# A graph layer with 640 hot edges of 1608 a part instead of 512 of 1532, and gathers that wait for a weighted copy three parts in front

## The chip, the cores and the metric

The kernel runs on one core of a Trainium2 chip. The metric is device time in microseconds (us) of one execution, and the number for a kernel is the median of three runs. The core has TensorE (PE, with its weight loads PEld), VectorE (DVE), ScalarE (ACT), GpSimd (POOL) and SyncE (SP); each takes its instructions in order. DMAs are issued from the queues of SP and POOL in what follows.

## The reference, cut to what matters

There are 12500 nodes with 128 features, and 412500 edges (`src`, `dst`), sorted by `dst`.

```python
theta = x[dst] - x[src]
w = sigmoid(relu(theta @ W1 + b1) @ W2 + b2)          # one gate an edge
agg = segment_sum(w * theta, dst)
indeg = segment_sum(ones, dst)
out = layernorm(x + agg + indeg * (x @ W4 + b4))
```

## The kernel before, in words

**Tables.** First a table `z` of 256 columns a node is written to DRAM: `x @ W1` and `x`. The edges are then taken in parts, in the order of `dst`. The first 18 parts (`PLAIN`) are of 1024 edges, whose rows are all gathered. Each later part has `CE` = 1532 edges, up to 1024 of them *cold* and up to 512 of them *hot*. Two parts make a block `b`; part `s` is half `h = s % 2` of block `s // 2`. There are 258 parts behind the plain ones, 18 to 275.

**Cold edges.** POOL gathers their rows of `z` with eight indirect DMAs of 128 rows a part (L401), into one of five buffers `zbuf`. DVE subtracts them from `y`, the rows of the destinations that PE has spread over the edges by a one-hot product (`spread_y`, L893, L951), multiplies by W2 (L956) and sums (L962). ACT makes the gate (L975) and the weighted copies into `wx` (L993).

**Hot edges.** The nodes up to 8192 are cut into 32 regions of 256 rows, four to a group. From each region a part takes at most 8 edges for each of its two lists, 512 in all, and their rows are not gathered but made by PE: DVE builds a one-hot tile `of` from the edges' places (`hot_tiles`, L1039), and PE multiplies it with three bf16 terms of the region's rows, which stay in SBUF (`hot_products`, L1055, 24 products for eight parts of a group). ACT copies the sums into a ring `xT` (`hot_out`, L1069). For part `t` PE then turns `xT` and adds the destinations' rows (`hot_turned`, L1105, L1106: 512 columns in the bank `pz`), ACT takes relu (L1111), PE makes the gates' sums with `hr` as weights and one column moving (`hot_rows`, L1119) and transposes `xT` (L1122), and ACT makes gates and weighted copies `wxh` (`hot_weights`, L1128, L1131).

**Sums.** PE adds cold and hot edges into a window of 104 nodes by one-hot products (L1158): `begin_block` in an odd part, `add_block` in an even one, which also takes the hot edges of both halves. `total`, `finish`, `own` and `normalize` close a block; the square root of the variance is taken for five blocks together (`LB`, L1269).

**Which edges are hot** is found on the chip (`place`, L500): for 64 parts together, DVE runs 32 rounds, one a region, each an eight-wide maximum and a replacement over lists of 767 numbers (L586, L589), and then sorts the rest together. It is a generator whose steps are fitted in behind the parts' own work by a credit (2.5 a part, 5.5 a plain part).

**Order.** The main loop `part(s)` writes PE, ACT, DVE and SP's instructions in the order in which they run; nothing reorders them. In part `s` PE does `hot_turned(s+1)`, `spread_y(s+2)`, `hot_rows(s+1)`, and then the block's sums and the 24 hot products in turns (`issue`). The gathers of part `s+3` are issued in `spread_ahead(s)`, and write the buffer that part `s-2` has left. `paced` is looked up by `gather` but is empty.

Of the kernel before, what the change touches and what calls it, by code (L numbers as in the profile page):

```python
# [9 lines left out]
F32 = mybir.dt.float32  # L10
# [10 lines left out]
P = 128  # L21
# [15 lines left out]
NW = 3  # L37
AHEAD = 4
LB = 5
# [11 lines left out]
HK = HR * HS  # L51
HQ = HK // P
HOT = P * HT
LEADS = tuple(range(8))
OPENING = ((0,), (1, 7), (2, 6), (3, 5), (4,))
NU = 4
# [7 lines left out]
CE = 1532  # L64
# [5 lines left out]
HKL = HR * HE  # L70
# [14 lines left out]
def gnn_resnorm(  # L85
# [49 lines left out]
    assert HK == P * G and 2 * AW + D + WB <= 512 and LW <= SW  # L135
# [65 lines left out]
    of_buf = const.tile([P, max(HT * RG * HB * HS, BE)], F32, name="of")  # L201
    of_half = [of_buf.bitcast(BF16)[:, i * HT * RG * HB * HS:(i + 1) * HT * RG * HB * HS] for i in range(2)]
# [32 lines left out]
    wx_buf = [const.tile([P, K, AW], F32, name=f"wx{i}") for i in range(NW)]  # L235

    def table_load(c):
        n0, np_, m = chunks[c]
        xt = wx_buf[c % NW].rearrange("p k d -> p (k d)")[:, :BE]
# [15 lines left out]
    for name, v in (("w2_r", W2), ("b4_r", b4)):  # L255
        rows[name] = const.tile([P, D], F32, name=name)
        nc.sync.dma_start(
            rows[name], bass.AP(tensor=v.tensor, offset=v.offset, ap=[[0, P], [1, D]]))
# [11 lines left out]
    iota_row = const.tile([P, P], F32, name="iota_row")  # L270
# [36 lines left out]
    for i, t in enumerate(y2_buf):  # L307
        nc.vector.memset(t, 0.0)
        for h in range(SUB) if i < NY else (1,):
# [44 lines left out]
    xT_all = const.tile([P, HX, HK], F32, name="xT")  # L354
    xT_flat = xT_all.rearrange("p j e -> p (j e)")
# [7 lines left out]
    assert late_at + 2 * NS <= HX * HK and WB + D <= 512  # L363
    hot_src = const.tile([P, NU, RG * HB * HS], F16, name="hot_src")
# [135 lines left out]
    def place(i, scratch, es, ed, bb, dp):  # L500
# [79 lines left out]
        tops = ep.tile([P, WL], F32, name="ed")[:, :HKL].rearrange("p (r e) -> p r e", e=HE)  # L580
        for r in range(HR):
# [3 lines left out]
            eight = tops[:, r, :]  # L585
            v.max(eight, left)  # L586
            v.tensor_scalar(eight, eight, FLOOR, None, op0=OP.max)
            yield "k"
            v.match_replace(left, eight, left, TAKEN)  # L589
            yield "k"  # L590
# [19 lines left out]
        yield "p"  # L610
        hrel = pp.tile([P, S2, HQ], BF16, name="hrel")
        pt = scratch()[:, :HQ * P].rearrange("p (q j) -> p q j", q=HQ)
        for q in range(HQ):
            nc.tensor.matmul(pt[:, q, :], hd[:, q * P:(q + 1) * P], ident_b, start=True, stop=True)
        yield "c"
        for q in range(HQ):
            for h in range(LISTS):
                a, e = max(h * HKL - q * P, 0), min((h + 1) * HKL - q * P, P)
                if a < e:
                    nc.scalar.activation(hrel[a:e, :, q], pt[a:e, q, h * S2:(h + 1) * S2], AF.Copy)  # L620
        hot_s = dram.tile([HR // RG, S2, LISTS, RG * HE], F16, name=f"hot_s{i}")
        rows_d = dram.tile([S2, RW], BF16, name=f"off_d{i}")
        for h, at in enumerate(lists):
            nc.sync.dma_start(hot_s[:, :n, h, :].rearrange("g p e -> p g e"),
                              hi[at].rearrange("p (g e) -> p g e", e=RG * HE))
            nc.sync.dma_start(
                rows_d[:n, BP:].rearrange("p (l m) -> p l m", l=LISTS)[:, h, :], far[at])
        hots[s0] = hot_s, hrel, n
        yield "s"
# [89 lines left out]
    with tc.manual_schedule(engines={SP}), tc.tile_pool(name="work", bufs=2) as wp, tc.tile_pool(  # L719
# [65 lines left out]
        def load_block(b):  # L785
            base = nc.values_load(base_b[0:1, b:b + 1], engines=[SP], min_val=0, max_val=N - WB,
                                  skip_runtime_bounds_check_because="base_b is at most N - WB")
            xw = wp.tile([P, D], F32, name="xw", bufs=5)
# [4 lines left out]
            if PLAIN <= b * SUB < PLAIN + NY * SUB:  # L793
                nc.vector.memset(y2[HALF:], 0.0)
            x2 = blocks[b]["x2"] = y2 if b >= W0 else x2_buf[b]
            for h in range(SUB):
# [5 lines left out]
                nc.sync.dma_start(to[h * HALF:h * HALF + SW, :], rows)  # L802
            if b * SUB >= PLAIN:
# [3 lines left out]
                for h in range(SUB):  # L807
                    nc.sync.dma_start(
                        to_all[h * HALF:(h + 1) * HALF, :],
                        rows_d[i + h:i + h + 1, :].to_broadcast([HALF, RW]))  # L810
# [71 lines left out]
        def spread_y(s):  # L882
# [3 lines left out]
            for k0 in range(0, K if s < PLAIN else J, J):  # L886
# [4 lines left out]
                d["y"].append(y)  # L891
                for j in range(J if s < PLAIN else pairs(s)):
                    nc.tensor.matmul(y[:, j, :], d["oh"][:, (k0 + j) * P:(k0 + j + 1) * P],  # L893
                                     y_of(s), start=True, stop=True)
# [73 lines left out]
        def lgh():  # L968

            return halves[1][:, :SUB * HQ].rearrange("p (i q) -> p i q", q=HQ)  # L970
# [41 lines left out]
        EP = RG * HS  # L1012
# [20 lines left out]
        def hot_tiles(f, x=0):  # L1033

            i0, g, i1, i = f
            w = (i1 - i0) * HS * RG
            of = hot_of(turn_of[0] % 2, x, w)
# [4 lines left out]
        def hot_products(f, x, pd, steps_of):  # L1042

            i0, g, i1, i = f
            w = (i1 - i0) * EP
            of = hot_of(turn_of[0] % 2, x, w)
            of = of.rearrange("p t (m r e) -> p t r m e", r=RG, e=HE)
            if not x:
                pd = ps_l.tile([P, G, P], F32, name="pd").rearrange("p g e -> p (g e)")
            bank, pd = pd, pd[:, x:x + w]  # L1050
            to = pd.rearrange("p (m r e) -> p r m e", r=RG, e=HE)
            for q in range(RG):
                for j in range(HT * TERMS):
                    i, t = divmod(j, HT)
                    steps_of.append(lambda q=q, i=i, t=t, j=j: nc.tensor.matmul(  # L1055
                        to[:, q], tabs[:, g, i, q, t, :], of[:, t, q], start=j == 0, stop=j == HT * TERMS - 1))
            return bank, pd

        def hot_out(f, pd):
# [699 lines left out]
```

## Time and profile before

| | |
|---|---|
| median of 3 runs | 2937.81 us (2935.55 to 2943.02) |
| profiled execution's own time | 2943.8 us |
| its span, first to last instruction | 2942.0 us |
| busy PE, DVE, ACT, POOL | 87%, 81%, 72%, 74% of the span |
| mean granted TensorE clock | 0.937 |

A line of the page's groups and of the list by line has: line, engine, operation, tiles out<-in, shapes, count | busy us, mean ns of one | idle time of the engine before it and what ended that. A line of the timeline has: start in us, length in us, engine, line, operation, tiles, shapes, count, and in brackets the idle time before it. A busy PE is not a PE at its peak: the ends of matmuls are modelled, so the starts of two groups tell better what a group takes. Each f32 matmul stands as two passes, a transpose as one.

### The profile page before, as it was taken

The numbers are of one execution on the slowest core, as the hardware profiler recorded it, in microseconds if no ns is written. First come the engines' busy times: TensorE is split into PE (matmuls) and PEld (weight loads), VectorE is DVE, ScalarE is ACT, GpSimd is POOL, SyncE is SP. The second block draws the span as 40 slices with busy tenths as digits, with TensorE's granted clock in tenths as the row PEclk, the third lists the DMA queues.
The fourth block names the chain that finished last, engine by engine and source line by source line (L and its number), as shares of the span: only waits on it lengthen the run. The fifth ranks groups of instructions, "written<-read, shape, count | busy, mean of one in ns | idle before, by whom it ended". The sixth has DMA issues, their size and how long they took to land.

```text
span 2942.0 us, 59129 instructions
## 1 busy us (share of the span) xinstructions
PE 2548.2 (87%) x18606; PEld 2012.3 (68%) x18606; DVE 2380.3 (81%) x4436; ACT 2123.8 (72%) x6416; POOL 2164.5 (74%) x2213
## 2 busy tenths in 40 slices
PE   6877899988888998998898888898998888888886
PEld 5656677777676777776776666676776666677764
DVE  7899699888957988888558888888568888888654
ACT  6365778767777777677777777776777777677776
POOL 4566777777777777777777777777777777777774
PEclk8688999989999999999999999999999999999998
DMA  8455555555554555554554545454554555555542
GB/s 285 151 153 123 142 139 138 140 135 137 140 146 134 137 140 140 133 141 135 143 150 133 135 133 141 132 141 134 143 142 128 140 132 141 133 138 141 141 134 77
DMA packets 239329, 413.58 MB, mean 141 GB/s; under 512 B 63423, under 2 KB 147226, under 8 KB 237470
## 3 DMA queue, kind: packets, MB, share of 16 engines
q0 software_dynamic: 105280, 286.93, 35.3%
q1 hardware_dynamic: 131756, 116.40, 15.3%
q10 hardware_dynamic: 1970, 6.40, 0.7%
q8 instruction: 148, 2.42, 0.3%
q14 instruction: 175, 1.43, 0.2%
HBM read 388.57 MB, written 20.94 MB: 139 GB/s over the span
## 4 chain that ended last, share of the span: by engine, by line
PE 38%; ACT 19%; DVE 15%; DMA 11%; issue 7%; POOL 1%; DVEq 0%; SPq 0%; ACTq 0%; POOLq 0%
PE pa L1158 14%; DMA zbuf<-z,src_i 10%; DVE zbuf L951 5%; PE y L893 5%; PE pd L1055 5%; ACT wx L993 5%; PE px L1119 4%; ACT wxh L1131 4%; PE pz L1105 3%; PE pz L1106 3%; PE pz L1122 3%; ACT oh L872 2%; ACT oh L873 2%; ACT xT L1069 1%; ACT a L1213 1%
## 5 line engine op out<-in xcount | busy, mean ns | idle before, releaser
L401 POOL DMA_INDIRECT zbuf<-z,src_i x2060 | 2018.5, 980 | 637.0 <-issue 236.6
L993 ACT ACTIVATE wx<-zbuf,wx 128x128 f32<-128x128 f32 x2060 | 630.2, 388 | 0.0
L1158 PE MATMUL pa<-wx,ow 128*104 128x260 f32 (+1 forms) x2284 | 628.4, 393 | 0.0
L893 PEld LDWEIGHTS y<-y,oh 128*128 128x128 f32 (+1 forms) x2156 | 276.1, 197 | 420.5 <-DVE zbuf L951 378.2
L1055 PEld LDWEIGHTS <-tabs 128*128 128x128 bf16 x6360 | 452.8, 101 | 124.2 <-issue 8.2
L951 DVE TENSOR_TENSOR zbuf<-y,zbuf 128x1024 f32<-128x1024 f32 x258 | 315.1, 1221 | 272.2 <-DMA zbuf<-z,src_i 270.9
L1055 PE MATMUL pd<-of,tabs 128*128 128x128 bf16 (+3 forms) x6360 | 535.2, 223 | 0.0
L1111 ACT ACTIVATE hr<-pz 128x512 f32<-128x512 f32 x258 | 152.9, 593 | 522.9 <-PE pz L1106 522.8
L893 PE MATMUL y<-y,oh 128*128 128x128 f32 (+1 forms) x2156 | 314.7, 291 | 228.7 <-DVE zbuf L951 220.6
L1158 PEld LDWEIGHTS pa<-wx,ow 128*104 128x104 f32 x2284 | 342.8, 179 | 40.6 <-issue 0.4
L962 DVE TENSOR_REDUCE lg<-zbuf 128x8 f32<-128x1024 f32 x273 | 329.8, 1208 | 13.2
L956 DVE SCALAR_TENSOR_TENSOR zbuf<-zbuf,fix 128x1024 f32<-128x1024 f32 x273 | 331.6, 1215 | 9.3
L1158 PE MATMUL pa<-wxh,owh 128*104 128x130 f32 x2064 | 329.0, 296 | 0.0
L1131 ACT ACTIVATE wxh<-pz,wxh 128x128 f32<-128x128 f32 x1032 | 295.2, 369 | 42.1 <-PE pz L1122 35.9
L1105 PE MATMUL pz<-xT,wni 128*128 128x512 f32 x516 | 278.5, 621 | 1.6 <-ACT wxh L1131 1.6
L1158 PEld LDWEIGHTS pa<-wxh,owh 128*104 128x104 f32 x2064 | 274.3, 186 | 0.0
L1119 PEld LDWEIGHTS px<-w_c,hr 128*128 128x128 f32 x2064 | 263.5, 200 | 7.8 <-ACT hr L1111 7.8
L1119 PE MATMUL px<-w_c,hr 128*128 128x1 f32 x2064 | 262.1, 248 | 5.6 <-ACT hr L1111 5.6
L1106 PE MATMUL pz<-oh,y 128*128 128x512 f32 x516 | 264.5, 594 | 0.1
L872 ACT ACTIVATE oh<-to_all,away,mine 128x512 f32<-128x512 bf16 (+1 forms) x257 | 213.6, 831 | 3.1 <-DMA to_all<-off_d 3.1
L1106 PEld LDWEIGHTS pz<-oh,y 128*128 128x128 f32 x516 | 98.2, 191 | 124.3 <-issue 123.4
L1122 PE MATMUL pz<-wni,xT 128*128 128x128 f32 x1032 | 176.3, 297 | 0.0
(304 smaller groups left out, 3595.8 us busy)
## 6 DMA issues: line engine op xcount, KB each, us to landing
to_all<-off_d SPq DMA_DIRECT2D x258, 128.0 KB
zbuf<-z,src_i POOLq DMA_INDIRECT x2060
hot_src<-hot_s SPq DMA_DIRECT2D x228, 128.0 KB
y<-z SPq DMA_DIRECT2D x270, 28.0 KB
xw<-in_x_dram SPq DMA_DIRECT2D x138, 52.0 KB
out_dram<-o SPq DMA_DIRECT2D x138, 52.0 KB
wx<-in_x_dram ACTq DMA_DIRECT2D x12, 512.0 KB
z<-zbuf SPq DMA_DIRECT2D x6, 1024.0 KB
```

The source lines that it names most:

```text
L401: ins = nc.gpsimd.indirect_dma_start(out=rows_of(s)[:, k, :], out_offset=None, in_=z if s >= NH else x, in_offset=IndirectOffsetOnAxis(ap= ...
L893: nc.tensor.matmul(y[:, j, :], d["oh"][:, (k0 + j) * P:(k0 + j + 1) * P], y_of(s), start=True, stop=True)
L951: nc.vector.tensor_sub(half, yy.to_broadcast([P, 2, n, D]), half)
L956: nc.vector.scalar_tensor_tensor(h[:, at, :], h[:, at, :], 0.0, w2.to_broadcast([P, n, D]), op0=OP.max, op1=OP.mult)
L962: nc.vector.tensor_reduce(lg[:, at, 0], h[:, at, :], AX.X, OP.add)
L993: weighed[0] = nc.scalar.activation(wx[:, k, :D], rows_of(s)[:, k, D:], AF.Copy, scale=wx[:, k, D:D + 1])
L1055: steps_of.append(lambda q=q, i=i, t=t, j=j: nc.tensor.matmul(to[:, q], tabs[:, g, i, q, t, :], of[:, t, q], start=j == 0, stop=j == HT * ...
L1105: nc.tensor.matmul(pz, wneg, xT, start=True, stop=False)
L1106: nc.tensor.matmul(pz, y_of(t), blocks[t // SUB]["oh"][:, BP:], start=False, stop=True)
L1119: nc.tensor.matmul(lgh()[:, t % SUB, q:q + 1], hr[:, at], w2_c, start=True, stop=True)
L1131: nc.scalar.activation(wx[:, q, :D], pz[:, q * P:(q + 1) * P], AF.Copy, scale=wx[:, q, D:D + 1])
L1158: return [lambda i=i, one=one, w=w: nc.tensor.matmul(to if len(w.shape) == 3 else to[:, 0, :], one, w, start=first and i == 0, stop=last a ...
```

## The change

`CE` goes from 1532 to 1608. One region in four has a second round of maxima, so a group has 5 instead of 4 times 8 places a list (`RU`), and a part 640 instead of 512 hot places (`HK`, five columns of 128 instead of four, `HQ`). There are 246 parts behind the plain ones (18 to 263) instead of 258, and four calls of `place` instead of five.

What follows from 640 columns, which no longer fit one bank of 512: `hot_turned` works on two banks of 320, and its destinations' rows come by two products of 64 rows each; relu is two instructions; the gates' sums are made with W2 spread over 32 columns as weights and `hr` moving, so that they lie in rows (`rowed`); a sigmoid over 256 columns and two transposes turn them back (`hot_gates`, `hot_gates_turned`), and ACT copies them out before the weighted copies. The second round's region has products of 256 instead of 128 columns, the last region lies in another bank and is copied by itself (`last_out`). `spread_y` uses 64 rows instead of 128 with zeros. The sums and the hot products no longer take turns. One region's list is longer, so `place` has 40 rounds over lists of 805. Buffers shrink to make room: `wx` 3 to 2, `hot_src` 4 to 3, `owh` 2 to 1, `xw` 5 to 4, `LB` 5 to 4.

The gathers of part `s+3` are issued at the end of part `s` and the first of the eight waits for ACT's last weighted copy of part `s` (`paced`); the other seven no longer wait for ACT themselves.

```diff
-CE = 1532
+CE = 1608
-HK = HR * HS
+HK = HR // RG * RU * HS
+ST = 32
...
-            eight = tops[:, r, :]
+            for _ in range(1 if r % RG else 2):
+                eight = tops[:, u, :]
...
-                nc.sync.dma_start(to[h * HALF:h * HALF + SW, :], rows)
+                for g in range(SUB) if b * SUB >= PLAIN else (h,):
+                    nc.sync.dma_start(to[g * HALF:g * HALF + SW, :], rows)
...
+                if s >= PLAIN:
+                    at = slice(s % SUB * HALF, (s % SUB + 1) * HALF)
+                    oh, rows = oh[at], rows[at]
...
-            nc.tensor.matmul(pz, wneg, xT, start=True, stop=False)
-            nc.tensor.matmul(pz, y_of(t), blocks[t // SUB]["oh"][:, BP:], start=False, stop=True)
+            banks = pz[:, :HKL], halves[1][:, :HKL]
+            for l, to in enumerate(banks):
+                nc.tensor.matmul(to, wneg, xT[:, l * HKL:(l + 1) * HKL], start=True, stop=False)
+            for l, to in enumerate(banks):
+                at = slice(l * HALF, (l + 1) * HALF)
+                nc.tensor.matmul(to, y_of(t)[at], oh[at], start=False, stop=True)
...
-                nc.tensor.matmul(lgh()[:, t % SUB, q:q + 1], hr[:, at], w2_c, start=True, stop=True)
+                nc.tensor.matmul(rowed(q), w2_c.to_broadcast([P, ST]), hr[:, at], start=True, stop=True)
...
+            nc.scalar.activation(parts[t]["hr"][:, :2 * P], pz[:, 2 * P:], AF.Sigmoid, bias=b2_c)
...
+            nc.tensor.transpose(pz[:, 2 * P:3 * P], gates[:, :P], ident)
+            for q in range(G, HQ):
+                at = slice((q - G) * ST, (q - G + 1) * ST)
+                newest[0] = nc.tensor.transpose(pz[:, 2 * P + q * ST:2 * P + (q + 1) * ST],
+                                                gates[at, P:2 * P], ident[at, at])
...
+            if PLAIN + AHEAD <= s + 3 < NS:
+                paced[s + 3] = weighed[0]
+                gather(s + 3)
```

On PE, in an odd part, from the turned hot edges to the first hot product; `pz`, `px`, `y` and `pd` are PSUM tiles, `wni` holds the negative W1 and the identity, `w_c` is W2, `tabs` the regions' terms. Before:

```order
L1105 MATMUL pz<-xT,wni 128x512
L1106 MATMUL pz<-oh,y_146 128x512
L893 MATMUL y<-y_149,oh 128x128 x4
L1119 MATMUL px<-w_c,hr 128x1 x4
L1122 MATMUL pz<-wni,xT 128x128 x4
L1170 LDWEIGHTS third
L1170 MATMUL pa<-b_t,third 104x128
L1171 MATMUL pa<-wts,xuT 104x128
L815 MATMUL pa<-wni,xw 128x104
L1158 MATMUL pa<-wx_78,ow 104x260
L1055 LDWEIGHTS tabs
```

Now:

```order
L1136 MATMUL pz<-xT,wni 128x320
L1136 MATMUL px<-xT,wni 128x320
L1139 MATMUL pz<-oh,y_147 128x320
L1139 MATMUL px<-oh,y_147 128x320
L910 MATMUL y<-y_142,oh 128x128 x4
L1153 MATMUL pz<-hr,w_c 32x128 x5
L1156 MATMUL pz<-wni,xT 128x128 x2
L1156 MATMUL px<-wni,xT 128x128 x3
L1082 LDWEIGHTS tabs
L1082 MATMUL pd<-of,tabs 128x16x16
```

The hot part works on two banks, the gates' products give 32 rows each, and all 24 hot products now stand ahead of the block's sums. Also on PE, what stands now between the last hot product and the next part (the two transposes of the gates, and an odd part's sums):

```order
L1082 MATMUL px<-of,tabs 128x128
L1165 MATMUL pz<-wni,hr 128x128
L1168 MATMUL pz<-wni,hr 128x32
L1216 LDWEIGHTS third
L1216 MATMUL pa<-b_t,third 104x128
L1217 MATMUL pa<-wts,xuT 104x128
L828 MATMUL pa<-wni,xw 128x104
L1205 MATMUL pa<-wx_78,ow 104x260 x4
L1136 MATMUL pz<-xT,wni 128x320
```

Only these sums lie between the gates' transposes and the next part's first product into the same bank. On ACT, in an odd part, from the hot gates to the next part's relu. Before:

```order
L1128 ACTIVATE wxh<-px,b_c 128x4
L1131 ACTIVATE wxh<-pz,wxh 128x128 x4
L1232 ACTIVATE sw<-a 104x2
L1234 ACTIVATE px<-xw,sw 104x128
L975 ACTIVATE wx_78<-lg,b_c 128x8
L979 ACTIVATE wx_78<-rel 128x4
L993 ACTIVATE wx_78<-zbuf_176,wx_78 128x128 x8
L1111 ACTIVATE hr<-pz 128x512
```

Now:

```order
L1175 ACTIVATE wxh<-pz 128x5
L1178 ACTIVATE wxh<-pz,wxh 128x128 x2
L1178 ACTIVATE wxh<-px,wxh 128x128 x3
L1097 ACTIVATE xT<-px 128x12x8
L1097 ACTIVATE xT<-px 128x4x8
L1278 ACTIVATE sw<-a 104x2
L1280 ACTIVATE xw<-xw,sw 104x128
L996 ACTIVATE wx_79<-lg,b_c 128x8
L1000 ACTIVATE wx_79<-rel 128x4
L1014 ACTIVATE wx_79<-zbuf_178,wx_79 128x128 x8
L1097 ACTIVATE xT<-pd 128x12x32
L1097 ACTIVATE xT<-pd 128x4x32
```

The relu follows behind these; one weighted copy and the four copies of hot sums have come ahead of it.

More of the change, by code (lines that the diff above doesn't have):

```diff
@@ L1156, in products @@
         def products(to, terms, first, last):
-            return [lambda i=i, one=one, w=w: nc.tensor.matmul(
-                to if len(w.shape) == 3 else to[:, 0, :], one, w,
-                start=first and i == 0, stop=last and i == len(terms) - 1) for i, (one, w) in enumerate(terms)]
+            for i, (one, w) in enumerate(terms):
+                newest[0] = nc.tensor.matmul(to if len(w.shape) == 3 else to[:, 0, :], one, w,
+                                             start=first and i == 0, stop=last and i == len(terms) - 1)
         def sums_of(b):
@@ L1185, in add_up @@
                 terms.append((blocks[b]["sh"][:WB, :WB], carry[0][:WB, :AW]))
-            issue(products(blocks[b]["pa"][:, 1:, :], terms, h == 0 and begin, h == 1 and end), [])
+            products(blocks[b]["pa"][:, 1:, :], terms, h == 0 and begin, h == 1 and end)
             if end:
```

231 lines of the change are left out of this document (133 added, 98 removed).

## The prediction

> **What bounds the kernel now.** I read the page's groups first, then the timeline of POOL, the windows, the waits, and the timelines of PE and ACT over two parts. The group that the page puts first is POOL's:
>
> ```profile
> L401 POOL DMA_INDIRECT zbuf<-z,src_i x2060 | 2018.5, 980 | 637.0 <-issue 236.6
> ```
>
> The timeline of POOL, in the main loop and in the plain parts, shows what its idle time is:
>
> ```profile
> 1448.38 0.95 POOL L401 DMA_INDIRECT zbuf<-z,src_i  x1 [0.30 <-issue]
> 1449.63 0.95 POOL L401 DMA_INDIRECT zbuf<-z,src_i  x1 [0.30 <-issue]
> ...
> 166.69 0.95 POOL L401 DMA_INDIRECT zbuf<-z,src  x1 [0.30 <-issue]
> 167.95 0.95 POOL L401 DMA_INDIRECT zbuf<-z,src  x1 [0.30 <-issue]
> ```
>
> Gathers start 1.25 us apart, 0.95 and then 0.30 that belong to every issue. With the mean of the group it is 0.98 + 0.30 = 1.28, and eight make 10.24 us a part. The windows agree, with DVE light or heavy and the clock low or full:
>
> ```profile
> 100.00:200.00 100.00, 79.01 (x376) 60.30 (x375) 92.55 (x191) 54.71 (x133) 66.99 (x65) 0.76 0.50 138
> ...
> 1500.00:1600.00 100.00, 85.42 (x614) 67.75 (x613) 67.40 (x129) 72.66 (x224) 76.22 (x78) 0.91 0.53 143
> 1600.00:1700.00 100.00, 87.35 (x679) 67.80 (x678) 89.65 (x154) 76.44 (x237) 76.84 (x77) 1.00 0.52 137
> ```
>
> (The pairs are PE, PEld, DVE, ACT, POOL; then the granted clock.) POOL issues 77 or 78 in 100 us whatever the others do: it never waits. The others wait for it, in the list of waits:
>
> ```profile
> PEld y L893 <- DVE zbuf L951: 378.2, 197, 9.7
> DVE zbuf L951 <- DMA zbuf<-z,src_i: 270.9, 138, 6.5
> ```
>
> The length of a part comes from the first and last start of the hot edges' first product, which stands once a part:
>
> ```profile
> L1105 PE MATMUL pz<-xT,wni x516: 591/594/1057, 290.3 to 2911.1; 128*128 128x512 f32 x172
> ```
>
> That is (2911.1 - 290.3) / 257 = 10.20 us, POOL's own pace. Outside these 257 intervals lie 2942.0 - 2620.8 = 321.2 us. So POOL bounds the main loop, and PE is the next: two parts in which it never waited, from the timeline of PE:
>
> ```profile
> 1518.08 1.08 PE L1105 MATMUL pz<-xT,wni 128*128 128x512 f32 x2
> 1518.99 1.02 PE L1106 MATMUL pz<-oh,y 128*128 128x512 f32 x2
> 1519.85 1.05 PE L893 MATMUL y<-y,oh 128*128 128x128 f32 x8
> 1520.74 1.01 PE L1119 MATMUL px<-w_c,hr 128*128 128x1 f32 x8
> 1521.61 0.63 PE L1122 MATMUL pz<-wni,xT 128*128 128x128 f32 x4
> 1522.09 0.39 PE L1158 MATMUL pa<-a,sh 104*104 104x130 f32 x2
> ...
> 1525.17 1.95 PE L1158 MATMUL pa<-wx,ow 128*104 128x260 f32 x8
> 1526.96 0.50 PE L1055 MATMUL pd<-of,tabs 128*128 128x128 bf16 x6
> 1527.29 1.08 PE L1105 MATMUL pz<-xT,wni 128*128 128x512 f32 x2
> ...
> 1531.37 0.22 PE L1170 MATMUL pa<-b_t,third 65*104 65x128 bf16 x1
> ...
> 1531.77 0.60 PE L1158 MATMUL pa<-wx,ow 128*104 128x260 f32 x2
> ...
> 1534.97 1.08 PE L1105 MATMUL pz<-xT,wni 128*128 128x512 f32 x2
> ```
>
> An even part takes 9.21 us and an odd one 7.68, 8.45 in the mean, at full clock by the window of these two:
>
> ```profile
> 1518.00:1535.00 17.00, 17.00 (x140) 13.82 (x137) 9.05 (x15) 12.06 (x39) 12.75 (x14) 1.00 0.70 173
> ```
>
> PE has 1.8 us a part to spare; the change is paid out of that. Where PE waits long the clock is granted lower (0.91 above). I count full clock, since these waits should go.
>
> **The change part by part.** *Twelve parts fewer.* 245 intervals instead of 257: at the old pace 12 x 10.20 = 122 us less. POOL's floor stays: the gathers of the plain parts above wait for one semaphore alone and are 1.26 us apart too, so dropping ACT's wait from seven of eight gains nothing.
>
> *PE a part*, from the starts above, at full clock. A pass of 512 columns takes 0.43, so one of 320 takes 0.27. Turned rows: 4 x 0.27 + 0.05 = 1.13 for 0.91, **+0.22**. Destinations' rows: 4 x 0.27 = 1.08 for 0.86, **+0.22**. Gates' sums: ten passes of 128 columns at 0.11 (0.89 for the eight of L893) for 0.87, **+0.23**. A fifth transpose (four take 0.48) **+0.12**, two for the gates **+0.17**. Hot products: six of 24 have 256 columns, 0.11 for 0.055 (six take 0.33, 1526.96 to 1527.29), **+0.33**; that they no longer take turns with the sums costs nothing, since they run at 0.055 in the groups above already. Hot sums: four passes more a block at 0.11, **+0.22** a part. Then the array changes its shape five times a part: full to 64 rows, to 32 columns, to full, to 32 rows, to full. Before it never does in the main loop, but in the first plain parts it does so at every matmul:
>
> ```profile
> 119.21 0.49 PE L917 MATMUL y<-wni,xT 128*128 128x128 f32 x2
> 119.62 0.49 PE L915 MATMUL y<-y,oh 64*128 64x128 f32 x2
> ```
>
> Two passes take 0.41 until the next pair starts instead of 0.22, so one change costs 0.19, and five **+0.95**. The row is of 64 against 128 rows; the 32-wide forms I price by it, as the nearest there is. The Trainium skill, "TensorEngine Tiling (Array Packing)", Key Properties, says that every change of tiling mode drains TensorE, not only this one. By that rule all five are paid; by the row alone two of them are, and the part would be 0.57 us shorter.
>
> The sum is +2.46: 10.91 us a part if everything on PE runs one behind the other. Two places can be shorter: the destinations' products use different halves of the array's rows, and the gates' sums different quarters of its columns. If one tile's first pass runs beside its neighbour's second, these are 3 and 6 steps: 0.81 and 0.66, together 0.71 less, 10.20. No row of before has two tiles side by side, so both stay as ends.
>
> *ACT*, which PE waits for. Here is an odd part's second half in the timeline of ACT:
>
> ```profile
> 1530.16 0.67 ACT L1069 ACTIVATE xT<-pd 128x192 f32<-128x192 f32 x2
> 1530.69 0.84 ACT L872 ACTIVATE oh<-to_all,away,mine 128x512 f32<-128x512 bf16 x1
> ...
> 1532.70 0.25 ACT L1128 ACTIVATE wxh<-px,b_c 128x4 f32<-128x4 f32 x1
> 1532.98 1.14 ACT L1131 ACTIVATE wxh<-pz,wxh 128x128 f32<-128x128 f32 x4
> 1533.99 0.22 ACT L1232 ACTIVATE sw<-a 104x2 f32<-104x2 f32 x1
> ...
> 1534.55 0.29 ACT L975 ACTIVATE wx<-lg,b_c 128x8 f32<-128x8 f32 x1
> ...
> 1534.88 2.45 ACT L993 ACTIVATE wx<-zbuf,wx 128x128 f32<-128x128 f32 x8
> 1537.23 0.57 ACT L1111 ACTIVATE hr<-pz 128x512 f32<-128x512 f32 x1
> ```
>
> In the changed order the weighted copies cannot start before the gates are turned back, and behind them stands all of this before the next relu. From the last gates' transpose on PE: 0.16 until its result is there (1518.99 + 1.02 against 1519.85), 0.28 gates, five copies at 0.25 = 1.26, last hot sums 0.20 (by the 0.53 of L1069 for 512 columns), 0.56 and 0.33 for own and gate, 2.35 for eight copies, 0.53 hot sums, relu of 640 columns 0.70: 6.37. PE meanwhile has, in an odd part, a change of shape 0.19, 0.40 (1531.37 to 1531.77), 1.79 of sums, then 1.13 + 0.19 + 1.08 or 0.81, 0.89 and 0.19: 5.86 or 5.59, and then needs the relu. It waits 0.51 or 0.78 a pair of parts, **0.26 or 0.39** a part. Behind an even part the sums are 2 us longer, and there is no wait. The square root comes on the same path:
>
> ```profile
> 1458.63 1.28 ACT L1269 ACT_TABLE_LOAD   x1
> ...
> 1460.13 0.58 ACT L1111 ACTIVATE hr<-pz 128x512 f32<-128x512 f32 x1
> ```
>
> 1.50 us, now once in four blocks, eight parts: **+0.19**. Before, the wait for POOL hid it.
>
> So a part is 10.91 + 0.26 + 0.19 = 11.36 us one behind the other, and 10.20 + 0.39 + 0.19 = 10.78 with overlap. I take 10.9, near the second: tiles on different rows or columns share no cell.
>
> *DVE* gets eight rounds more a call of `place`, from the list by line:
>
> ```profile
> L586 DVE MAX8 ed<-ew 128x8 f32<-128x767 f32 x160 | 153.1, 957 | 4.3 <-PE px L762 0.3
> L589 DVE MATCH_REPLACE8 ew<-ed,ew 128x767 f32<-128x767 f32 x160 | 150.6, 941 | 0.0
> ```
>
> 8 x (0.96 + 0.94 + 0.3 of small ones) = 17.6, and lists 5% longer some 6 more: 24 us a call. The first call stands in the plain parts, where DVE is 93% busy: **+24 us** on the path. Later calls are spread over some 57 parts, DVE then stands near 9.2 us a part, under 10.9. The lower end for the 24 is 0.
>
> *Free.* The wait of the gathers, on POOL, where only later gathers queue behind it. An odd part's subtraction on DVE's timeline, and a gather's landing in the chain that ended last:
>
> ```profile
> 1526.83 1.22 DVE L951 TENSOR_TENSOR zbuf<-y,zbuf 128x1024 f32<-128x1024 f32 x1 [4.97 <-DMA zbuf<-z,src_i]
> ...
> 1533.52 2.79 DMA zbuf<-z,src_i
> ```
>
> That part's copies end at 1537.23, 10.4 us behind its subtraction. The subtraction three parts on comes 30.6 us behind it at POOL's pace; less 2.8 of landing and 10.2 of gathers, POOL comes to those gathers 17.6 us behind it. The wait costs nothing until ACT is 7 us later than now. SP gets four more DMAs a block; DMA engines stand at 0.53, loads have two parts in hand, and nothing but output queues behind them. Fewer buffers of `wx`, `owh`, `hot_src` each leave about a part of room.
>
> *Sum.* 321.2 + 24 + 245 x 10.9 = 3016 us of span, +2.5% on 2942.0. The profiled execution's own time is 1.8 us over its span and 0.2% over the median: 3011 us.
>
> **Rivals.** (1) *PE fits under POOL*: tiles run wholly side by side and the 32-wide changes cost little. Then 10.24 rules, 321 + 24 + 245 x 10.24 = 2854, 2850 on the median's scale: 3% faster. It decides when PE with its waits is under 10.24, that is 0.54 below my lower sum. For it: the 0.95 for changes rests on one kind of row. Against it: ACT's chain gets longer relative to PE whenever PE gets shorter, so that 0.55 less on PE gains only some 0.3. Chance 0.20. The Trainium skill, "TensorE: Matmul & The Clock Gate", Part 3, gives the span of packed tiles as one matmul and some 4 ns a tile. By that rule the two places are 0.54 and 0.44 and the part 10.43, some 2897 us; no row here shows it. (2) *In between*, 10.35 to 10.63 a part, 2880 to 2945: 0.12, of which 0.05 is within 0.3% (about what a measurement can tell from no change; 10.56 to 10.63). (3) *Worse*: the 32-column tiles cannot load weights ahead and each pass takes 0.21, as the first pass behind a change does now: +1 us a part, 3260. Chance 0.06. (4) Too many edges of a part do not fit, and the kernel falls back on its general branch behind the flag: far slower, and no trace prices it. 0.02.
>
> **How the numbers follow.** Forecast (10.63 to 11.4) 0.60, and the rivals 0.20, 0.12, 0.06, 0.02. Faster: 0.20 + 0.07 = 0.27; same 0.05; slower 0.60 + 0.08 = 0.68. The range goes from rival 1 at 2850 to 11.4 us a part at 3135. The forecast's own is 2945 to 3135.
>
> **What would show it.** Right: POOL idle between groups of eight, not only 0.30 a gather; PE's waits for L951 gone and waits for relu in every second part; PE's clock nearer 1; 0.41 for two passes behind each change of shape; the first hot product near 314 us. Wrong: POOL still at 78 in 100 us (rival 1), or gates' sums over 1.5 us (rival 3).

## The result and the profile after

The changed kernel takes 3086.4 us (median of 4 runs, 3081.6 to 3093.4), the kernel before beside it 2939.5: a ratio of 1.0502 (95% interval 1.0479 to 1.0526), slower, twice the 2.5% that the forecast of 3011 us stood for. The profiled execution's own time is 3093.4 us, its span 3091.6. Twelve of the eighteen experiments' runs fell on chips where TensorE was granted less clock and the kernel before itself took 4037 to 4122 us; a ratio is always to the kernel before on the same chip.

The length of a part again comes from the first and last start of the hot edges' first product (here L1136), from the list by source line; then POOL's gathers, from the groups by shape:

```profile
L1136 PE MATMUL pz<-xT,wni x492: 432/432/741, 333.1 to 3060.5; 128*128 128x320 f32 x164
```

```profile
L405 POOL DMA_INDIRECT zbuf<-z,src_i x1962 | 1884.6, 961 | 884.3 <-issue 516.9 <-ACT wx L1014 306.7 <-ACT src_i L723 19.7
```

(3060.5 - 333.1) / 245 = 11.13 us a part, where the forecast has 10.9. The main loop takes 2727.4 us, 106.6 more than before, the stretch ahead of it 42.8 more (333.1 against 290.3), the tail the same 31. A gather still takes 0.96 + 0.30; POOL no longer sets the pace. The windows show where the time is (pairs of PE, PEld, DVE, ACT, POOL, then the granted clock): with `place` running, right behind it, and in the last 71 parts, where there is no `place` to do:

```profile
1500.00:1600.00 100.00, 88.64 (x684) 70.47 (x684) 78.11 (x131) 74.50 (x237) 64.69 (x69) 0.90 0.48 129
1600.00:1700.00 100.00, 91.95 (x739) 73.06 (x737) 58.77 (x96) 85.03 (x278) 73.64 (x78) 0.98 0.53 142
1700.00:1800.00 100.00, 61.47 (x462) 48.41 (x461) 45.60 (x94) 55.16 (x176) 46.58 (x48) 0.80 0.34 95
2400.00:2500.00 100.00, 93.61 (x766) 74.35 (x764) 59.92 (x96) 83.82 (x274) 74.31 (x79) 0.98 0.54 146
```

In the rows without `place` POOL issues 78 or 79 gathers in 100 us, as before the change; in the first, with it, 69. Taken by part, from the starts of L1136: 141 parts in which `place` works on VectorE take 11.46 us in the mean, the last 71 take 10.42. The third row holds one stall of 26.5 us. The list of waits names the engine:

```profile
DVE a L1270 <- ACT xuT L833: 408.8, 109, 8.2
POOL zbuf L405 <- ACT wx L1014: 306.7, 141, 29.2
PEld y L910 <- DVE zbuf L968: 272.3, 120, 10.1
PE y L910 <- DVE zbuf L968: 211.3, 120, 9.6
```

```profile
PE pz L1153 <- ACT hr L1145: 33.4, 30, 2.7
...
DVE zbuf L968 <- DMA zbuf<-z,src_i: 11.3, 29, 1.5
```

PE's wait for VectorE's subtraction is there as before, but the subtraction no longer waits for a gather (11.3 us, 270.9 before): VectorE itself is late. `finish` (L1270) waits for `total` on ACT 408.8 us, 51.6 before:

```profile
DVE a L1224 <- ACT xuT L820: 51.6, 21, 6.3
```

VectorE's timeline over a pair of parts with `place` (L968 is a part's subtraction, L689 the first of a place step, L1298 begins `normalize`):

```profile
1502.85 1.22 DVE L968 TENSOR_TENSOR zbuf<-y,zbuf 128x1024 f32<-128x1024 f32 x1
...
1511.04 1.21 DVE L968 TENSOR_TENSOR zbuf<-y,zbuf 128x1024 f32<-128x1024 f32 x1
...
1519.45 0.29 DVE L1270 TENSOR_TENSOR a<-a,pa 104x130 f32<-104x130 f32 x1 [4.12 <-ACT xuT L833]
1519.66 1.24 DVE L1187 TENSOR_TENSOR owh<-fix,hrel 128x1040 f32<-128x1040 f32 x1
...
1521.40 0.69 DVE L689 TENSOR_SCALAR px<-ew 128x512 int32<-128x512 int32 x1
...
1524.98 0.28 DVE L1298 TENSOR_TENSOR xw<-xw,a 104x128 f32<-104x128 f32 x1
...
1526.39 1.22 DVE L968 TENSOR_TENSOR zbuf<-y,zbuf 128x1024 f32<-128x1024 f32 x1
```

From 1502.85 to 1526.39 is 23.54 us, 11.8 a part. The first window below is this stretch, the second the time right behind the wait of TensorE that is shown next:

```profile
1502.85:1526.39 23.54, 22.27 (x156) 17.75 (x156) 18.80 (x33) 12.93 (x47) 13.11 (x14) 0.81 0.41 113
1504.10:1508.00 3.90, 3.88 (x22) 3.21 (x23) 3.90 (x6) 0.16 (x1) 2.84 (x3) 0.50 0.58 167
```

VectorE is busy for 18.80 us (9.4 a part, near the 9.2 of the prediction), and 4.12 are a wait in the middle of the odd part, with five microseconds of work queued behind it (1519.66 to 1524.98) that needs nothing of what ACT is late with. TensorE's timeline over the same stretch shows the other side:

```profile
1504.12 2.07 PE L910 MATMUL y<-y,oh 64*128 64x128 f32 x8 [5.40 <-DVE zbuf L968]
1506.12 1.06 PE L1153 MATMUL pz<-hr,w_c 128*32 128x128 f32 x10
...
1511.44 0.39 PE L1165 MATMUL pz<-wni,hr 128*128 128x128 f32 x1
...
1511.94 0.47 PE L1205 MATMUL pa<-a,sh 104*104 104x130 f32 x2
...
1516.22 0.70 PE L1136 MATMUL pz<-xT,wni 128*128 128x320 f32 x2
...
1517.39 0.53 PE L1139 MATMUL pz<-oh,y 64*128 64x320 f32 x1
1517.40 0.53 PE L1139 MATMUL px<-oh,y 64*128 64x320 f32 x1
...
1518.04 1.05 PE L910 MATMUL y<-y,oh 64*128 64x128 f32 x8
1519.02 0.62 PE L1153 MATMUL pz<-hr,w_c 128*32 128x128 f32 x10
1519.58 0.44 PE L1156 MATMUL pz<-wni,xT 128*128 128x128 f32 x2
...
1521.84 0.28 PE L1165 MATMUL pz<-wni,hr 128*128 128x128 f32 x1
...
1522.22 0.26 PE L1216 MATMUL pa<-b_t,third 65*104 65x128 bf16 x1
...
1524.42 0.70 PE L1136 MATMUL pz<-xT,wni 128*128 128x320 f32 x2
```

L910 waits 5.40 us for the late subtraction. Behind the wait the same steps from L910 to L1165 take 7.32 us (1504.12 to 1511.44), which take 3.80 without one (1518.04 to 1521.84): the granted clock is 0.50 in the window behind the wait. The Trainium skill says that the clock falls to half behind an idle window of some 3.4 us ("TensorE: Matmul & The Clock Gate", Part 1, What's actually happening), and the trace agrees. So TensorE comes late to L1136, ACT late to relu and to `total` behind it, and VectorE waits for `total`: a loop through three engines. PE alone would need less than the gathers: from one L1136 to the next it takes 8.20 us where it never waits (1516.22 to 1524.42), 2.20 of them for the sums of an odd part (from 1522.22). An even part's sums take 4.28 (1511.94 to 1516.22), so the other interval is 10.28, and the mean 9.24.

### The profile page after: what moved, and what is told of

Read it like the earlier page. It is cut to its first block, busy times and chain, and to the rows that moved or that the text cites. A ratio compares the mean times of both kernels' runs of the same rounds, so it can differ in the third digit from the quotient of the medians.

```text
span 3091.6 us, 61930 instructions
## 1 busy us (share of the span) xinstructions
PE 2687.5 (87%) x20496; PEld 2134.5 (69%) x20496; DVE 2299.2 (74%) x4117; ACT 2314.2 (75%) x7325; POOL 2027.8 (66%) x2115
## 4 chain that ended last, share of the span: by engine, by line
PE 46%; ACT 19%; DVE 17%; issue 6%; POOL 6%; DMA 6%; DVEq 0%; SPq 0%; ACTq 0%; POOLq 0%
PE pa L1205 12%; PE pd L1082 9%; POOL zbuf L405 6%; PE y L910 6%; ACT wx L1014 5%; ACT wxh L1178 4%; PE pz L1153 4%; DVE zbuf L968 4%; DMA zbuf<-z,src_i 4%; PE pz L1156 2%; PE px L1156 2%; PE pz L1139 2%; PE px L1082 2%; DVE ew L596 2%; DVE ed L593 2%
## 5 line engine op out<-in xcount | busy, mean ns | idle before, releaser
L910 PE MATMUL y<-y,oh 64*128 64x128 f32 x2058 | 307.1, 294 | 224.1 <-DVE zbuf L968 211.3
L910 PEld LDWEIGHTS y<-y,oh 64*128 64x128 f32 x2058 | 278.5, 201 | 309.9 <-DVE zbuf L968 272.3
L1082 PE MATMUL pd<-of,tabs 128*128 128x256 bf16 (+3 forms) x4554 | 428.1, 255 | 0.0
L1270 DVE TENSOR_TENSOR a<-a,pa 104x130 f32<-104x130 f32 x123 | 35.7, 290 | 410.7 <-ACT xuT L833 408.8
L979 DVE TENSOR_REDUCE lg<-zbuf 128x8 f32<-128x1024 f32 (+1 forms) x261 | 314.9, 1207 | 12.9
L973 DVE SCALAR_TENSOR_TENSOR zbuf<-zbuf,fix 128x1024 f32<-128x1024 f32 (+1 forms) x261 | 316.7, 1214 | 8.9
L968 DVE TENSOR_TENSOR zbuf<-y,zbuf 128x1024 f32<-128x1024 f32 x246 | 299.6, 1218 | 13.1 <-DMA zbuf<-z,src_i 11.3
L885 ACT ACTIVATE oh<-to_all,away,mine 128x640 f32<-128x640 bf16 (+1 forms) x245 | 215.6, 880 | 27.2 <-DMA to_all<-off_d 27.2
L1178 ACT ACTIVATE wxh<-px,wxh 128x128 f32<-128x128 f32 x738 | 218.0, 377 | 0.0
L1153 PE MATMUL pz<-hr,w_c 128*32 128x128 f32 x2460 | 174.8, 307 | 33.5 <-ACT hr L1145 33.4
L1139 PE MATMUL pz<-oh,y 64*128 64x320 f32 x492 | 198.0, 482 | 4.3 <-ACT oh L886 4.3
L1139 PE MATMUL px<-oh,y 64*128 64x320 f32 x492 | 198.0, 482 | 0.0
L1298 DVE TENSOR_TENSOR xw<-xw,a 104x128 f32<-104x128 f32 x132 | 37.5, 284 | 210.0 <-ACT xw L1280 210.0
```

The costliest lines, as they stand in the source:

```text
L885: nc.scalar.activation(oh, blocks[b]["to_all"][:, c0:c1], AF.Abs, scale=mine, bias=away)
L910: nc.tensor.matmul(y[:, j, :], oh[:, (k0 + j) * P:(k0 + j + 1) * P], rows, start=True, stop=True)
L968: nc.vector.tensor_sub(half, yy.to_broadcast([P, 2, n, D]), half)
L973: nc.vector.scalar_tensor_tensor(h[:, at, :], h[:, at, :], 0.0, w2.to_broadcast([P, n, D]), op0=OP.max, op1=OP.mult)
L979: nc.vector.tensor_reduce(lg[:, at, 0], h[:, at, :], AX.X, OP.add)
L1082: newest[0] = nc.tensor.matmul(to, tabs[:, g, i, q, t, :], of[:, t, :, e0:e1], start=j == 0, stop=j == HT * TERMS - 1)
```

## The experiments

The theories: **A**, the loop through VectorE sets the pace where `place` runs. **B**, the gathers' new wait for ACT does. **C**, PE and ACT's chain is longer than the gathers' pace by itself, as predicted. The first four ran side by side with a kernel before at 2940.0 us.

**1. Without the gathers' wait.** `gather(s + 3)` goes back into `spread_ahead`, and nothing is put into `paced`:

```diff
                 spread_y(s + 2)
+                if PLAIN + AHEAD <= s + 3 < NS:
+                    gather(s + 3)
...
-                paced[s + 3] = weighed[0]
-                gather(s + 3)
```

> The changed kernel without its wait of the gathers: a part's gathers are issued behind the products of the y rows again, and none of them waits for ScalarE's last weighted copy. Theory A (a loop through VectorE in the stretches where place runs sets the pace: in odd parts VectorE waits in finish for ScalarE's total, does the place steps only then, and comes late to the next subtraction): POOL's waits for ScalarE (306.7 us in the list of waits) are only where the lateness shows, so the time stays within 0.5% of the changed kernel, 3071 to 3102 us; the gathers go on waiting, now for the buffer that they write. Theory B (the new wait holds the gathers back, and they hold the rest): 2% to 5% faster, 2935 to 3025 us. Theory C (TensorE and ScalarE alone are longer than a gather's pace, as predicted): within 0.5%.

3070.8 us, ratio 1.0446 (1.0428 to 1.0464). From its list of waits:

```profile
POOL zbuf L405 <- ACT wx L1014: 357.0, 466, 27.6
```

The gathers wait for ACT in total longer than with the wait (306.7), now through the buffer that they write. The wait costs 16 us of the 147, half a per cent: just past the edge of what A said, and far from B.

**2. The place steps in front of finish**, in the odd part:

```diff
             if done_b:
+                spend("kxm")
                 finish(b - 1)
```

> The changed kernel with the place steps of an odd part that only VectorE works on put in front of finish instead of behind it, so that they fill VectorE's wait for ScalarE's total. Nothing is added or left out. Theory A (loop through VectorE): the parts with place fall from 11.46 us towards the 10.4 of the last 71 parts without it, 141 x 0.7 to 1.05 less: 2940 to 2990 us. Theory B (the gathers' wait) and theory C (TensorE and ScalarE alone): the same time, 3071 to 3102 us.

3012.4 us, ratio 1.0248 (1.0231 to 1.0266): 74 us less than the changed kernel by the order of VectorE alone. Neither B nor C allows that. The gain is smaller than A said, and the mean part 10.81 us (332.3 to 2980.6). The parts with `place` take 10.92 us instead of 11.46, the last 71 the same 10.42:

```profile
DVE a L1270 <- ACT xuT L833: 261.5, 62, 7.4
PEld y L910 <- DVE zbuf L968: 206.2, 115, 10.1
```

**3. total in front of the relu**, so that `finish` finds it done:

```diff
+            if done_b:
+                total(b - 1)
             if t < NS:
                 hot_turned(t)
...
-            if done_b:
-                total(b - 1)
```

> The changed kernel with total's two copies on ScalarE (which read what TensorE finished a part earlier) put in front of the hot sums' copies and the relu, so that finish on VectorE no longer waits behind the relu. VectorE's order is the same. Theory A: finish's wait (408.8 us in 109 times, 3.7 each) falls by the products and the relu that no longer stand in front, some 2.5 us in each odd part with place, 70 x 2 to 2.5 us: 2915 to 2960 us. Theory B and theory C: the same within 0.5%, since what is moved is two short copies; by C 0.5 us a pair slower at most.

3015.7 us, ratio 1.0263 (1.0246 to 1.0281), 71 us less. The same wait is shortened from its other end; that is the loop cut at ACT instead of at VectorE. The parts with `place` take 10.92 us here too. Again the gain is smaller than A said:

```profile
DVE a L1270 <- ACT xuT L833: 155.4, 73, 5.3
PEld y L910 <- DVE zbuf L968: 238.8, 120, 10.1
```

**4. The changed kernel without the later place.** `turns = {}`, and `set_of` and `hot_set` always give the first 64 parts' lists.

> The changed kernel without the main loop's three calls of place and the loads for them: all later parts use the lists of the first 64 again. It leaves out the placement of the parts from 82 on. Theory A: every main part runs as the last 71 do now, 10.42 us, and the one stall of 26.5 us goes with the loads: 321 + 43 + 245 x 10.3 to 10.45 = 2885 to 2925 us. Theory C: TensorE and ScalarE's chain stays, 10.9 us a part and more, 3030 us or above.

2895.6 us, ratio 0.9852 (0.9836 to 0.9869). (2862.1 - 333.6) / 245 = 10.32 us a part:

```profile
L1136 PE MATMUL pz<-xT,wni x492: 432/432/537, 333.6 to 2862.1; 128*128 128x320 f32 x164
```

That is inside A's range, and theory C's 10.9 us are out: the main loop without `place` runs near the gathers' pace, and the three later calls with their loads cost the changed kernel 199 us of main loop (2727.4 against 2528.5), the part with the stall of 26.5 among them. The waits have not gone:

```profile
DVE a L1270 <- ACT xuT L833: 565.8, 121, 8.4
PEld y L910 <- DVE zbuf L968: 192.7, 121, 4.4
```

VectorE waits in `finish` even longer than in the changed kernel, and PE waits 1.6 us at a time for the subtraction, 2.3 there. So it isn't the wait by itself that costs the 199 us, but the wait with `place` queued behind it.

**5. The kernel before without the later place**, by the same edit. It was run four times, on three chips; the first three times the clock was 0.84 and the kernel before took 4037, 4041 and 4122 us.

> The kernel before without its main loop's calls of place and their loads (all later parts use the lists of the first 64). It leaves out the placement of the parts from 82 on. Theory A, in which place costs something only where VectorE's loop is longer than the gathers' pace: before, POOL sets the pace at 10.2 us, in the parts with place 10.34 and without 9.76 to 10.2, so 0 to 35 us less: 2905 to 2940 us, beside the 165 us that the changed kernel lost by place without its stall. Rival (place costs the kernel before as much, so that the 5% are something else): 2800 us or below.

3953.2 us, ratio 0.981 (0.976 to 0.987).

> The kernel before without its main loop's calls of place and their loads, once more, since TensorE's granted clock was 0.84 in the first run, below every profile so far, and the kernel before took 4037 us beside it. It leaves out the placement of the parts from 82 on. Theory A: POOL sets the kernel before's pace with and without place: 0 to 35 us less than the kernel before, 2905 to 2940 us. Rival (place costs the kernel before as much as the 165 us that it costs the changed one, stall aside): 2800 us or below.

3950.7 us, ratio 0.976 (0.971 to 0.981).

> The kernel before without its main loop's calls of place and their loads (all later parts use the lists of the first 64), at the clock of the first four runs if it is granted. It leaves out the placement of the parts from 82 on. Theory A, in which POOL sets the kernel before's pace with and without place: 0 to 35 us less than the kernel before. Rival (place costs the kernel before as much as the changed one, 165 us): 140 us less or more.

3924.2 us, ratio 0.953 (0.945 to 0.961). None of these three bears on the gathers' pace: POOL is busy 53% or 54% of the span in them, 74% in the kernel before.

> The kernel before without its main loop's calls of place and their loads (all later parts use the lists of the first 64). It leaves out the placement of the parts from 82 on. Theory A, in which POOL sets the kernel before's pace with and without place, at a granted clock of 0.93 or more: 0 to 35 us less than the kernel before. Rival (place costs the kernel before as much as the changed one, 165 us): 140 us less or more.

2902.6 us beside 2941.6, ratio 0.9865 (0.9847 to 0.9884): `place` costs the kernel before 39 us, four more than A's bound, where it costs the changed one about five times that (3086.4 against 2895.6). Its list of waits shows what took its place:

```profile
DVE zbuf L951 <- DMA zbuf<-z,src_i: 710.0, 203, 6.0
```

VectorE merely waits longer for gathers (270.9 us with `place`).

**6. The stall.** The last set of the changed kernel has 53 whole parts, and SP loads 53 rows. In the stall TensorE waits for ACT, and ACT for `to_all`, which SP loads behind these rows:

```profile
ACT oh L885 <- DMA to_all<-off_d: 27.2, 1, 27.2
```

The timeline of SP there, and that of the kernel with the loads as 48 rows and 5:

```profile
1697.94 5.89 SPq L188 DMA_DIRECT2D ed<-in_dst_dram  x2
1703.88 14.63 SPq L191 DMA_DIRECT2D ed<-in_dst_dram  x1
...
1735.21 0.51 SPq L818 DMA_DIRECT2D to_all<-off_d  x1
```

```profile
2403.36 1.44 SPq L190 DMA_DIRECT2D es<-in_src_dram  x4
...
2405.19 1.39 SPq L190 DMA_DIRECT2D ed<-in_dst_dram  x4
2406.62 0.25 SPq L194 DMA_DIRECT2D ed<-in_dst_dram  x1
```

```diff
-                nc.sync.dma_start(t[h * S2:h * S2 + full, :m], ...[[CE, full], [1, m]]
+                for a, e in ((0, full // 16 * 16), (full // 16 * 16, full)):
+                    nc.sync.dma_start(t[h * S2 + a:h * S2 + e, :m], ...[[CE, e - a], [1, m]]
```

> The changed kernel with the loads of the last set's 53 rows made as 48 rows and 5. In the trace of the changed kernel the 212 packets of the 53-row loads run one behind the other from 1698 to 1731 us at 0.13 us each, where 256 packets of another set's 64-row loads are through in 5 us; SyncE is held in issuing them, and the one stall of 26.5 us stands there. If it is the count of rows that puts them on one queue, the stall goes and the time falls by 22 to 27 us: 3059 to 3065 us. Rival (they are slow because the memory or the gathers are busy there, or the stall is another's): no change.

The 212 packets of these loads take 32.2 us from first to last in the changed kernel (0.13 us each, one at a time) and 4.9 in this one, SP's queue is not held (0.25 us for the last of them), and no part takes over 24.2 us at a mean of 16.8, where one took 37.3 at a mean of 11.1. The Trainium skill, "DMA: Bandwidth & Descriptors", Why a DMA increments its semaphore by 16 and not by 1, has a copy go out on the largest number of engines up to 16 that divides its slowest dimension: 1 for the prime 53, 16 for 48. The trace agrees: by the packets' times 0.9 of the 212 is under way on average in the changed kernel, 8.1 in this one. The gain in time isn't measured: this kernel ran at a clock of 0.80, on a chip where the kernel before takes 4036.9 us, at 4513.3 (1.119).

**7. Both edits and the loads** (2, 3 and 6 together).

> The changed kernel with three things together: the odd part's place steps that only VectorE works on in front of finish, total in front of the relu, and the last set's loads as 48 rows and 5. Theory A: the first two work on one and the same wait, so they don't add up: one gives 71 to 74 us, both 85 to 110, and the loads 24: 2950 to 2980 us. If they were two separate costs they would add to 145, and with the loads it would be 2917.

4505.1 us beside 4036.9, ratio 1.118 (1.112 to 1.124).

> The changed kernel with the odd part's place steps in front of finish, total in front of the relu, and the last set's loads as 48 rows and 5, once more, for the same reason. Theory A (the first two work on one wait): 2950 to 2980 us. Rival (two separate costs): 2917 us.

4509.5 us beside 4041.5, ratio 1.115 (1.112 to 1.118).

> The changed kernel with the odd part's place steps in front of finish, total in front of the relu, and the last set's loads as 48 rows and 5. Theory A (the first two work on one wait), at a granted clock of 0.91 or more: 2950 to 2980 us. Rival (two separate costs): 2917 us.

4455.9 us beside 4099.4, ratio 1.087 (1.078 to 1.095), at a clock of 0.80 each time. Whether the 74 and 71 us are one and the same wait stays open.

**8. All of VectorE's waits off the path.** The edits of 7, no wait of the gathers, and `normalize` moved behind the logits of the next even part, where ACT's product has long been made (with a fifth buffer for `xw`, one for `sh`):

```diff
             if done_b:
                 spend("kxm")
                 finish(b - 1)
+            if h == 0 and PLAIN // SUB <= b - 1 <= NK:
+                normalize(b - 2)
...
-            if done_b:
-                normalize(b - 1)
```

> The same three things, and normalize moved from the end of the odd part behind the logits of the next even part (a fifth buffer for xw, one for sh), where the product that it waits for on ScalarE (278.9 to 375.6 us in the lists of waits) is long there; and the gathers' wait for ScalarE left out, worth 16 us by itself. Theory A: VectorE's last wait in an odd part goes, place then costs what VectorE has free, and the parts come to 10.3 to 10.5 us as without place: 321 + 43 + 245 x 10.3 to 10.5 = 2890 to 2940 us. Rival (VectorE's order is not what is left): 2940 to 2965 us.

4112.3 us beside 4036.9, ratio 1.020 (1.014 to 1.026).

> The three things of the last kernel, normalize behind the next even part's logits, and no wait of the gathers for ScalarE, once more. Theory A: 2890 to 2940 us. Rival (VectorE's order is not what is left): 2940 to 2965 us.

4102.5 us beside 4041.5, ratio 1.016 (1.013 to 1.019).

> The changed kernel with the odd part's place steps in front of finish, total in front of the relu, normalize behind the next even part's logits, the last set's loads as 48 rows and 5, and no wait of the gathers for ScalarE. Theory A, at the clock of the first four runs: 2890 to 2940 us, 0.98 to 1.00 of the kernel before. Rival (VectorE's order is not what is left): 1.00 to 1.01.

4025.5 us beside 4122.2, ratio 0.980 (0.973 to 0.988). On the chip that ran both it gains some 400 us against kernel 7 (4112.3 against 4505.1, 4102.5 against 4509.5); which of its two further edits does that was not tried.

> The changed kernel with the odd part's place steps in front of finish, total in front of the relu, normalize behind the next even part's logits, the last set's loads as 48 rows and 5, and no wait of the gathers for ScalarE. Theory A, at a granted clock of 0.93 or more: 2890 to 2940 us, 0.98 to 1.00 of the kernel before. Rival (VectorE's order is not what is left): 1.00 to 1.01.

2919.7 us beside 2941.6, ratio 0.9937 (0.9916 to 0.9958): 0.6% faster than the kernel before, and inside A's range. 10.42 us a part (331.0 to 2883.2). Its list of waits:

```profile
DVE a L1273 <- ACT xuT L836: 338.0, 63, 11.2
...
PE pz L1156 <- ACT hr L1148: 108.8, 116, 1.5
...
PEld y L913 <- DVE zbuf L971: 26.0, 3, 8.7
```

The loads of 53 rows are mended in this kernel too, and no part takes over 22.2 us. VectorE still waits in `finish`, but PE's wait for VectorE is gone (272.3 us in the changed kernel), and the main loop is 24 us longer than that of kernel 4 (2552.2 against 2528.5), where the changed kernel's is 199 longer. The 24 are not the whole price of `place` here, since the edits also gain where there is none: the last 71 parts take 10.18 us, 10.35 in kernel 4. By 245 x 10.18 = 2494 an estimate of the price is 58 us; kernel 8 without `place` was not run. What PE waits for most now is the relu, in 116 of 246 parts, as predicted.

**9. Place spread more evenly** (VectorE takes up ACT's first result a part later; nine steps counted at 4 us).

> The kernel before this one in the list, with place's work spread more evenly: VectorE does not wait in the same step for the two activations that place hands to ScalarE (6.8 us in each of the three calls, in the trace with place in front) but takes up the result a part later, and the last nine steps of a call (where VectorE's place work is up to 8 us in one part) count as 4 us instead of 2.5, at 3.0 us a part. Theory A: 10 to 30 us faster than the kernel before this one. Rival (it is not VectorE's order any more): the same within 5 us.

4108.4 us beside 4041.5, ratio 1.016 (1.013 to 1.019), as kernel 8 on that chip.

> The kernel that ran at 2920 us, with place's work spread more evenly: VectorE takes up the result of place's first two activations a part later instead of waiting for them (8.2 us on TensorE in each of the three calls), and the last nine steps of a call count as 4 us instead of 2.5, at 3.0 us a part. Theory A, at a granted clock of 0.93 or more: 10 to 30 us faster, 2890 to 2910 us. Rival (it is not VectorE's order any more): 2915 to 2925 us.

4025.8 us beside 4099.4, ratio 0.982 (0.975 to 0.990). No gain over kernel 8 shows; at a clock of 0.93 it was not seen.

## Why the prediction was wrong

The sign, the bound of the kernel before and several prices held; the size did not, and the 10.9 us a part was near the measured 11.13 for other reasons.

- **The step that failed**: "Later calls are spread over some 57 parts, DVE then stands near 9.2 us a part, under 10.9." The work is 9.4 in the pair above, but the sum was held against the part's length as if VectorE could use its time whenever. It works in order, and in an odd part it stands 4 us in `finish` with place steps queued behind. Work and wait make 11.8. The clue was in the order alone: `total` stands behind the relu, and the relu's instructions had just been moved and lengthened. The prediction asked only what ACT does to PE. Shown by 2, 3 and 4: 74, 71 and 199 us. Nor are the calls spread over 57 parts: the three work in 141, 47 each, with 3.9 us of `place` a part on VectorE, where the kernel before has 3.3 (four calls in 194 parts). Two points of the change that its section does not name work the same way: the credit goes from 2.5 to 2.8 a part (5.5 to 6.5 in a plain part), and the one-hot tile `owh` (L1187, 1.24 us) moves from the even part to the odd one, behind `finish`. What either is worth was not tried.
- **Clock**: "I count full clock, since these waits should go." They did not go; the granted clock is 0.911, 0.937 before, and behind the wait shown above 3.80 us of PE work took 7.32.
- **PE's sum** was too high. The change adds 0.8 us a part (9.24 against 8.45), not 1.75 to 2.46. Turned rows and destinations' rows take 1.82 together (1516.22 to 1518.04) instead of 2.13 to 2.40, the gates' sums 0.56 (1519.02 to 1519.58) instead of 0.66 or 1.10. The tiles run side by side, more so than in the prediction's shorter end with its three and six steps: the products for `pz` and `px` start 10 ns apart. The Trainium skill's rule that it cited ("TensorE: Matmul & The Clock Gate", Part 3) gives 0.54 for the destinations' rows and 0.44 for the gates' sums; measured are 0.65 (1517.39 to 1518.04) and 0.56, each with a change of shape in it. And the five changes of shape at 0.19 were priced about twice too high: without any, and with the tiles wholly side by side, the prediction's prices from L1136 to the gates' transposes are 1.13 + 0.54 + 0.89 + 0.44 + 0.60 + 1.65 + 0.17 = 5.42 us, the trace has 6.00 (1516.22 to 1522.22), and so an estimate of one change is 0.1. Transposes (0.60), gates' transposes (0.38 against 0.36) and hot products were as priced. PE's own work, 9.24, is under the gathers' pace, but rival 1 asks that of PE with its waits, and these kept the part at 11.13, and at 10.32 without `place`.
- **ACT's relu**: 33.4 us in PE's waits above, where 64 to 96 were forecast. In kernel 8, with VectorE out of the way, it is 108.8. It had been covered, not absent.
- **The plain part**: +24 for the first `place` agrees with VectorE's busy time, 231.1 against 206.6 us in these two windows. But the stretch is 42.8 us longer, since VectorE also stands idle 18 us more, and the first hot product comes at 333.1 us, not near 314; the two longest of its waits are below, behind the windows of after and of before. The prediction put none there. It also read POOL at 77 or 78 gathers in 100 us throughout; of the three windows that it shows, the one in the plain parts has 65.

```profile
60.00:333.10 273.10, 191.80 (x1061) 152.40 (x1060) 231.11 (x458) 123.34 (x302) 139.00 (x143) 0.72 0.45 129
```

```profile
60.00:290.30 230.30, 181.43 (x1066) 143.35 (x1064) 206.59 (x426) 125.72 (x302) 136.72 (x137) 0.77 0.53 149
```

```profile
DVE px L657 <- ACT tabs L1124: 7.6, 1, 7.6
DVE zbuf L965 <- PE y L910: 7.6, 2, 7.4
```

- **Free**: the gathers' wait was called free and costs 16 us. SP was called free, "loads have two parts in hand"; the count of rows in the last set was not looked at, and the loads of 53 rows held one part up for 26.5 us.

The account of the main loop, by the experiments: without `place` the change gives 48 us (2528.5 against 2576.6, from 292.6 to 2869.2 in kernel 5); `place` takes 155 more than it did (199 against 44). That is the +107.

## What to carry to other kernels

Don't compare an in-order engine's work with the length of a stage; walk its queue and add the waits, because work queued behind a wait can't fill it. Where filler work (here `place`) stands behind a wait, the repair is to put it in front: here that and its like, with the wait of the gathers left out and the loads of 53 rows mended, were worth 167 us and turned 5% slower into 0.6% faster. When one engine stops being the bound, ask of every wait that it had hidden who is late next.

## What the runs showed of the hardware

On three of the five chips of the experiments the kernel before took 37% to 40% longer, at a mean granted clock of 0.81 to 0.84, and TensorE paused for over a microsecond between two matmuls of one group, for nothing that the profile shows, as in the kernel of 6 (timeline of PE):

```profile
2009.25 3.62 PE L1208 MATMUL pa<-wxh,owh 128*104 128x130 f32 x17 [1.16 <-issue]
```

The cause was not found. Where TensorE does not pause it can run as fast as on the other chips: in the same trace the steps from the turned rows to the odd part's sums take 6.01 us (2014.45 to 2020.46), and 6.00 in the changed kernel's. On these chips the kernels of 6 and 7 lose 9% to 12%, and kernel 8 loses or gains 2%. POOL is busy 45% of the span in the kernel of 6, and the chain that ended last lies on TensorE for 46% of it and on POOL for none, so it isn't the gathers that set the pace there. A ranking by half a per cent on one chip need not hold on another: kernel 8 was at 0.994, 1.020, 1.016 and 0.980.
